# A message-passing layer: full tables carry their surplus rows into the next table, keys of pairs are computed earlier, and leftovers of pairs are ranked in front of the next group's second layer

## The chip, the cores and the metric

The kernel runs on one core of one Trainium2 chip. The metric is the device time in microseconds (us) of one execution. Besides the tensor engine (PE, whose loading of weights is listed as PEld), the core has the vector engine (DVE), the scalar engine (ACT), GpSimd (POOL) and the queue engine SP, which here only issues transfers. Every engine works through its own instructions strictly in order, and engines wait for each other on semaphores. Transfers are issued from SP, ACT and POOL.

## The reference, cut to what matters

```python
h = jnp.maximum(_layernorm(x, axis=-1), 0.0)              # x: 12500 x 128
# inside the layer; idx_i = src (unsorted), idx_j = dst (sorted), 400000 edges
h = h @ W_in2f.T
Wij = smu(f_ij @ W_f1.T + b_f1) @ W_f2.T + b_f2            # f_ij: 400000 x 20
Wij = Wij * rcut_ij[:, None]
x_ij = h[idx_j] * Wij                                      # one message of 128 numbers an edge
agg = jax.ops.segment_sum(x_ij, idx_i, num_segments=h.shape[0])
out = smu(agg @ W_o1.T + b_o1) @ W_o2.T + b_o2             # added to x
```

Each edge makes a message from the node row at its `dst` end and from a two-layer filter of its 20 attributes; messages are summed at the `src` end. Edges come sorted by `dst`, so the rows to gather lie close together, and the places to sum into are scattered.

## The kernel before, in words

Edges are cut into 3125 tiles of 128; four tiles are a **group** (782 groups), two groups a super-group. The main loop takes one step a group and is software-pipelined: step p does for group p+1 the second layer (`weigh`, on PE, tile `pw`) and the product with the gathered rows (`mix`, on DVE, tile `ms`), for p+2 the gather by one-hot product (`gather` on PE, `take` on ACT, tile `hg`), and for p+3 the first layer (`hide`, `bend`). The order on each engine is the order in which the code names the calls; nothing reorders it.

**Slots.** The messages are not summed at once. They are scattered into a table in device memory and read back. Nodes are cut into 98 bins of 128 nodes; a table has `CAP` rows for each bin, each of 129 floats: the message and the node's place in its bin. Row by row, the slot is the count of earlier rows of the same bin: `bins` marks and adds counts (DVE), `count` forms running counts by products with triangular matrices (PE, tile `pc`), `read` takes them out (DVE), `number` adds the bin's start to give the index `ix` (DVE). `places_in` (ACT, L1086) writes the places into the last column of `ms`. Then POOL issues one indirect transfer for each tile of 128 rows (`scatter_rows`, L1110). A message tile is reused once its transfers have landed; there are 9 of them.

**Pairs.** In about every 2.5th group the four tiles are taken as two against two. `number` makes `key` for them (L812), `spread_keys` turns two of its columns on PE (L830), `match` compares (DVE, L838), and rows of the same bin are put side by side by a product (`permute`, PE, L875), so that one descriptor writes two rows: 2 transfers instead of 4. What found no partner is ranked by `rank_left` (PE, L848 and L849) and `place_left` (DVE, L855 and L856), packed into one tile `lt`, and sent with a later **host** group as a fifth transfer, whose bins are counted there too (`bins`, L724 and L725).

**Epochs.** The groups are cut into ten epochs (`PARTS`, in super-groups), each with its own table. During an epoch, the table of the epoch before is fetched from SP (`fetch`, L1141, four chunks ahead), a one-hot is built of the place column (`choose`, DVE, L1155), and each 128 rows are multiplied by it (`add`, PE, L1168), a bin's products accumulating; `Q` = CAP/128 such slices a bin, summed into `agg`. Three stores in memory are used in turn. A store has to hold zeros, or rows that cannot be mistaken, where nothing was written: before their first use the parts of the bins that may stay empty are filled with zeros (`clear`, L226, from SP), and reuse is told apart by an offset added to the places (`mark_round`). The tables are sized so that each alone holds its fullest bin: CAP is 768, 768, 768, 768, 640, 512, 384, 384, 256, 128, thus Q is 6, 6, 6, 6, 5, 4, 3, 3, 2, 1, 42 in all.

The groups of the last two epochs are computed in between the others (every ninth super-group, from the second epoch on) and kept in memory; they are scattered at the very end from these rows (`kept_rows`). An alarm count (`bad`) sends the program into a slow general path if a table was too small.

## Time and profile before

| what | value |
|---|---|
| median of 3 runs | 3832.49 us (3823.35 to 3832.53) |
| the profiled execution, as a whole | 3826.85 us |
| its span, first to last instruction | 3825.1 us |
| mean granted clock of PE | 0.964 |
| PE, PEld, DVE, ACT, POOL busy | 3294.2, 2872.9, 3116.8, 2839.2, 2855.5 us |
| device memory read, written | 500.66 MB, 398.23 MB |
| scatters (indirect transfers from POOL) | 2902 |

Times in the trace are of the span. A busy share is an average over all stages; a wait is listed with what ended it last. In the groups of instructions the columns are busy time, mean ns of one, and the engine's idle time before them with what ended it. Matmuls overlap, so the mean of one is longer than what it adds to the engine's busy time. Scatters in order show where the epochs lie: the first scatter of the second epoch starts at 614 us, of the third at 1189, of the fourth at 1735 and of the fifth at 2282 us.

### The profile page before, as it was taken

What the parts mean: (1) busy time and instruction counts of PE and PEld (TensorE: products, weight loads), DVE (VectorE), ACT (ScalarE), POOL (GpSimd) and SP (SyncE); (2) the same over time, 40 slices, a digit from 0 to 9 for tenths busy, and PEclk for the clock granted to TensorE, in tenths of its full rate; (3) what the DMA queues carried; (4) which work ended last, traced back from release to release, by engine and by line L of the source; (5) the groups of instructions that cost most, each with busy time, mean ns of one, the idle gap of its engine ahead of it and who ended that gap; (6) DMA issues with size and microseconds to landing.
All of it is one profiled execution on the core that took longest, in us unless ns stands there. A gap on an engine that the chain in (4) does not pass through costs nothing.

```text
span 3825.1 us, 90354 instructions
## 1 busy us (share of the span) xinstructions
PE 3294.2 (86%) x28066; PEld 2872.9 (75%) x28066; DVE 3116.8 (81%) x8275; ACT 2839.2 (74%) x7986; POOL 2855.5 (75%) x2946
## 2 busy tenths in 40 slices
PE   8777776988888999999989889999999889997767
PEld 4346665877777888878878778888888888887657
DVE  7878976877777888888888888888898888886657
ACT  7767766878888888888888888888778777875102
POOL 6777777777767777777777777777777777777776
PEclk9989988999999999999999999999999999999889
DMA  5888888888888878888878878888888888886977
GB/s 156 231 236 239 236 230 233 248 251 246 263 253 232 238 227 231 244 239 235 229 222 232 235 214 242 253 239 247 232 244 249 233 235 246 241 236 177 312 247 228
DMA packets 663936, 905.06 MB, mean 237 GB/s; under 512 B 179875, under 2 KB 462631, under 8 KB 663321
## 3 DMA queue, kind: packets, MB, share of 16 engines
q1 hardware_dynamic: 556025, 666.99, 63.5%
q0 software_dynamic: 100112, 219.93, 17.8%
q10 hardware_dynamic: 7312, 12.29, 0.9%
q8 instruction: 228, 3.74, 0.4%
q14 instruction: 259, 2.12, 0.2%
HBM read 500.66 MB, written 398.23 MB: 235 GB/s over the span
## 4 chain that ended last, share of the span: by engine, by line
PE 33%; DMA 18%; DVE 16%; ACT 11%; issue 11%; POOL 9%; SPq 2%; ACTq 0%; DVEq 0%; POOLq 0%
DMA buf<-ms,ix 12%; PE pg L1168 10%; POOL buf L1110 9%; PE pw L998 6%; PE pt L875 5%; ACT hg L973 3%; PE pc L752 3%; DVE se L1155 3%; DVE mt L838 2%; DVE ms L1040 2%; ACT oh L634 2%; ACT ge L926 2%; PE ph L954 2%; PE pw L1000 1%; DVE pc L796 1%
## 5 line engine op out<-in xcount | busy, mean ns | idle before, releaser
L1110 POOL DMA_INDIRECT buf<-ms,ix x2516 | 2444.3, 971 | 813.6 <-issue 569.0
L1168 PE MATMUL pg<-se,rw 128*128 128x128 f32 x8036 | 1168.7, 284 | 107.8 <-DVE se L1155 61.2
L1168 PEld LDWEIGHTS pg<-se,rw 128*128 128x128 f32 x8036 | 1037.2, 194 | 166.4 <-issue 65.5
L973 ACT ACTIVATE hg<-ph,w_sb 128x128 f32<-128x128 f32 x2784 | 781.9, 361 | 94.5 <-PE ph L954 80.4
L998 PE MATMUL pw<-w_f,ge 128*128 128x128 f32 x5568 | 779.2, 284 | 30.5 <-DVE ms L1040 14.3
L998 PEld LDWEIGHTS pw<-w_f,ge 128*128 128x128 f32 x5568 | 697.5, 197 | 50.0 <-issue 23.7
L1155 DVE TENSOR_TENSOR se<-irow_ps,rw 128x1536 f32<-128x1536 f32 (+1 forms) x345 | 587.4, 1703 | 112.1 <-DMA rw<-buf 89.5
L634 ACT ACTIVATE oh<-rbc,nrow 128x512 bf16<-128x512 uint8 x725 | 538.6, 743 | 33.5 <-DMA rbc<-rel_dram 33.1
L635 ACT ACTIVATE oh<-oh,onesb 128x512 bf16<-128x512 bf16 x743 | 536.0, 721 | 24.2
L796 DVE TENSOR_REDUCE pc<-pc 128x4 f32<-128x392 f32 (+1 forms) x782 | 466.4, 596 | 81.0 <-PE pc L752 77.4
L1040 DVE TENSOR_TENSOR ms<-pw,hg 128x512 f32<-128x512 f32 x482 | 330.2, 685 | 137.8 <-DMA buf<-ms,ix 36.5
L875 PE MATMUL pt<-ms,mt 128*128 128x129 f32 x2676 | 345.0, 279 | 55.0 <-DVE at L855 48.2
L875 PEld LDWEIGHTS pt<-ms,mt 128*128 128x128 f32 x2676 | 319.1, 193 | 66.7 <-issue 23.3
L752 PE MATMUL pc<-eo,tri 128*128 128x392 f16 x782 | 261.5, 334 | 69.8 <-DVE ix L818 46.8
L954 PE MATMUL ph<-hw,oh 126*128 126x128 bf16 x2784 | 274.4, 221 | 39.0 <-ACT hg L973 36.0
L926 ACT ACTIVATE ge<-pu 128x512 f32<-128x512 f32 x451 | 272.9, 605 | 17.4 <-PE pu L918 15.5
L752 PE MATMUL pc<-so,ones_h 128*128 128x392 f16 (+1 forms) x996 | 279.4, 306 | 0.1
L1000 PE MATMUL pw<-wls,f 128*128 128x128 bf16 x2784 | 274.2, 222 | 0.0
L1088 ACT ACTIVATE ms<-lo_b,mark 128x4 f32<-128x4 uint8 x309 | 91.3, 295 | 231.9 <-DVE ms L1040 219.7
L1110 POOL DMA_INDIRECT buf<-lt,ix x214 | 203.3, 950 | 78.0 <-issue 27.7
L954 PEld LDWEIGHTS <-oh 126*128 126x128 bf16 x2784 | 217.0, 99 | 52.5 <-issue 44.3
L752 PEld LDWEIGHTS <-ones_h 128*128 128x128 f16 x1554 | 151.8, 98 | 139.2 <-issue 17.1
(344 smaller groups left out, 5313.0 us busy)
## 6 DMA issues: line engine op xcount, KB each, us to landing
rw<-buf SPq DMA_DIRECT2D x292, 774.0 KB
f<-f_parts SPq DMA_DIRECT2D x370, 240.0 KB
buf<-zero SPq DMA_DIRECT2D x146, 387.0 KB
rbc<-rel_dram SPq DMA_DIRECT2D x389, 128.0 KB
buf<-ms,ix POOLq DMA_INDIRECT x2516
f_parts<-hs SPq DMA_DIRECT2D x105, 360.0 KB
rw<-buf SPq DMA_DIRECT2D x49, 645.0 KB
f_parts<-hs SPq DMA_DIRECT2D x107, 240.0 KB
```

Source lines behind the costliest of these rows:

```text
L634: nc.scalar.activation(oh, loaded[s][1][:, o:o + n], AF.Abs, bias=pneg if s < FEW // SUP else nrow)
L635: nc.scalar.activation(oh, oh, AF.Relu, scale=-1.0, bias=onesb[:, 0:1])
L752: nc.tensor.matmul(to, by, of, start=start, stop=stop, skip_group_check=True)
L796: nc.vector.tensor_reduce(sl[:, :n], pc[:, :n], op=ALU.max, axis=AX.X)
L875: nc.tensor.matmul(po[:, j * (ROW + 1):j * (ROW + 1) + w], pp[:, o:o + P], ms[:, i, ROW:ROW + w], start=(i == 0), stop=(i == 1))
L954: nc.tensor.matmul(ph[:, j * P:(j + 1) * P], oh[:3 * WIN, a:a + P], hw[:3 * WIN, g % PER, :], start=True, stop=True)
L973: nc.scalar.activation(hg[:, j * P:(j + 1) * P], rows_of[g][:, j * P:(j + 1) * P], AF.Copy, scale=w_sb[:, t + j:t + j + 1])
L998: nc.tensor.matmul(pw[:, a:a + P], ge[:, a:a + P], w_f2, start=(a == 0), stop=False, skip_group_check=True)
L1040: nc.vector.tensor_tensor(ms[:, :n, 0:P], pw.rearrange("p (j f) -> p j f", f=P)[:, :n], hg.rearrange("p (j f) -> p j f", f=P)[:, :n], op=A ...
L1110: i = nc.gpsimd.indirect_dma_start(out=(wide if g in host or g in pair_no else bufs)[k][:, :], out_offset=bass.IndirectOffsetOnAxis(ap=ix, ...
L1155: nc.vector.tensor_tensor(se[:, a:a + n], own.unsqueeze(1).to_broadcast([P, n, P]), rows_in[c][:, a:a + n, P:P + 1].to_broadcast([P, n, P] ...
L1168: nc.tensor.matmul(pgs[0][:, g, :], rows_in[c][:, o, 0:P], sel[c][:, o, :], start=(q == 0), stop=(q == Q[k] - 1))
```

## The change

**Tables.** The ten tables are now chains (`CHAINS`, of 5, 3, 1 and 1). In a chain, a bin's part of table k+1 lies right behind its part of table k in one store (`store`, 98 bins of S = 3200 rows). A bin that is full in epoch k goes on in the rows of table k+1: the slot is limited by `LIM`, the room of both tables, and the counts of the next epoch begin with what went over (`carry`, from one more product in `limits_of`). So only the end of a chain has to hold the fullest bin. CAP becomes 640, 640, 640, 640, 640, 512, 384, 384, 256, 128 and Q 5, 5, 5, 5, 5, 4, 3, 3, 2, 1, 38 in all; `PARTS` is rebalanced. The first five tables have rows of their own and are all cleared before use, 192, 192, 192, 256 and 256 rows a bin (before: three tables, 384 rows a bin each), each within the first three quarters of the epoch before it. The second chain reuses the rows of the first three tables. Waits between scatters, clears and fetches are now given by hand (`apart`, `behind_all`).

**Pairs.** `number` of a pair runs right behind `read` in the step before. `rank_left` and `place_left` of a pair run in the following step, in front of `weigh` and behind it. `rank_left` has one more product, which adds the constant `spot`, so that the subtraction L855 is gone; the comparison now reads `falling` and the product's bank. In a host group, one scalar-tensor-tensor operation takes the place of L724 and L725. Pairs are 224 instead of 223, scatters 2901 instead of 2902.

**Message tiles.** A plain group's tile is now made as 128 x 4 x 129 (`message_tile`) and a pair's as 128 x 2 x 259 (`pair_tile`); before, one flat tile was viewed in both ways.

```diff
-PARTS = (59, 58, 58, 58, 47, 37, 27, 24, 16, 7)
+PARTS = (58, 55, 54, 53, 48, 42, 33, 25, 16, 7)
+CHAINS = (5, 3, 1, 1)
...
+    for i, n in enumerate(CHAINS):
+        a = len(CAP)
+        ends = [0]
+        for k in reversed(range(a, a + n)):
+            ends.insert(0, max(ends[0] + 1, math.ceil(sum(rows_for(k, a + n)) / P)))
+        caps = [(u - v) * P for u, v in zip(ends, ends[1:])]
+        at_ = 0 if i <= 1 else OFF[-1] + CAP[-1]
+        for j, c in enumerate(caps):
+            CAP.append(c)
+            OFF.append(at_ + sum(caps[:j]))
+            LIM.append(c + (caps[j + 1] if j + 1 < n else 0))
...
+    store = dram.tile([NB + SPARE, S, ROW], F32, name="buf")
+    rows_at = store.rearrange("b s r -> (b s) r")
...
             if g in first:
-                nc.vector.memset(before, 0.0)
+                if carried(first[g]):
+                    nc.vector.tensor_scalar(before, carry, BIG, None, op0=ALU.min)
+                else:
+                    nc.vector.memset(before, 0.0)
...
                 if g in host:
-                    lot = cnt.tile([P, NB], F16, name="el")
                     rows_of_bins(k)
-                    nc.vector.tensor_scalar(lot, bin_row, left_of[host[g]][1], None, op0=ALU.is_equal)
-                    nc.vector.tensor_add(then, whole, lot)
+                    lot = then
+                    nc.vector.scalar_tensor_tensor(then, bin_row, left_of[host[g]][1], whole, op0=ALU.is_equal, op1=ALU.add)
...
+                if carried(k + 1):
+                    on_one = bank_of[:, 1, :NB]
+                    nc.tensor.matmul(on_one, one_h, after, start=True, stop=True)
+                    nc.vector.tensor_scalar(carry, on_one, -float(CAP[k]), 0.0, op0=ALU.add, op1=ALU.max)
...
-            nc.tensor.matmul(at_, tri, met_of(g, 0, 2), start=True, stop=False, skip_group_check=True)
+            nc.tensor.matmul(at_, ident, spot, start=True, stop=False, skip_group_check=True)
+            nc.tensor.matmul(at_, tri, met_of(g, 0, 2), start=False, stop=False, skip_group_check=True)
             nc.tensor.matmul(at_[:, 1:2], ones_h, met_of(g, 0), start=False, stop=True, skip_group_check=True)
...
-            at_ = cnt.tile([P, 2], F32, name="at")
-            nc.vector.tensor_tensor(at_, spot, kt[:, 2 * P:2 * P + 2], op=ALU.subtract)
             nc.vector.tensor_tensor(pp[:, 4 * P:].rearrange("p (j e) -> p j e", j=2),
-                                    irow_ps.unsqueeze(1).to_broadcast([P, 2, P]),
-                                    at_.unsqueeze(2).to_broadcast([P, 2, P]), op=ALU.is_equal)
+                                    falling.unsqueeze(1).to_broadcast([P, 2, P]),
+                                    kt[:, 2 * P:2 * P + 2].unsqueeze(2).to_broadcast([P, 2, P]), op=ALU.is_equal)
...
         def message_tile():
-            return msg.tile([P, 2 * (2 * ROW + 1)], F32, name="ms")
+            return msg.tile([P, GRP, ROW], F32, name="ms")
...
+        def pair_tile():
+            return msg.tile([P, 2, 2 * ROW + 1], F32, name="ms")
...
+                for j in range(FIRST):
+                    if (j == 0 and g >= BY) or 0 < j <= k or (j == k + 1 and is_clean(g)):
+                        behind_all(i, after_clear[j])
+                    else:
+                        apart(i, f"cleared{j}")
...
-            elif k + 1 < BUFS:
+            elif k + 1 < FIRST and cleared < len(cleans):
                 past = BY if k == 0 else 0
-                upto = min(len(cleans), -(-(i + 1 - past) * len(cleans) // (ng - 4 - past)))
+                upto = min(len(cleans), -(-(i + 1 - past) * len(cleans) // (by_group[k] - g0 - 2 - past)))
...
             step()
-            number(at(p + 1))
+            if at(p + 1) not in paired:
+                number(at(p + 1))
+            if g in paired:
+                rank_left(g)
             weigh(at(p + 1))
+            if g in paired:
+                place_left(g)
...
             read(at(p + 2))
+            if at(p + 2) in paired:
+                number(at(p + 2))
             parts(hi)
-            if at(p + 1) in paired:
-                rank_left(at(p + 1))
-                place_left(at(p + 1))
```

How the rows of the program stand now, at three places. A row is line, operation, written tile and what it reads, and what it waits for; `DMASW` are landings of POOL's transfers, `DMAHW` of SP's and ACT's, the others are engines. First ACT, around two plain groups and a pair. Before:

```order
L1036 ACTIVATE ms<-lo_b 128x2x2 [waits DMASW6_49,DMASW5_49,DVE_49]
L1037 ACTIVATE ms<-hic,shift 128x2
L973 ACTIVATE hg<-ph,w_sb 128x128 [waits PE_49]
L973 ACTIVATE hg<-ph,w_sb 128x128 x3
L926 ACTIVATE ge<-pu 128x512 [waits PE_49]
L634 ACTIVATE oh<-rbc,nrow 128x512 [waits DMAHW4_49]
L635 ACTIVATE oh<-oh,onesb 128x512 [waits Activation_49]
L1180 ACTIVATE agg<-pg_15306 128x512 [waits PE_49]
L1090 ACTIVATE ms<-lo_b 128x4 [waits DMASW2_49,DMASW1_49,DMASW7_49,DMASW0_49,DVE_49]
L973 ACTIVATE hg<-ph,w_sb 128x128 [waits PE_49]
```

and now:

```order
L1059 ACTIVATE ms<-lo_b 128x2x2 [waits DMASW3_49,DMASW2_49,DVE_49]
L1060 ACTIVATE ms<-hic,shift 128x2
L1000 ACTIVATE hg<-ph,w_sb 128x128 [waits PE_49]
L1000 ACTIVATE hg<-ph,w_sb 128x128 x3
L953 ACTIVATE ge<-pu 128x512 [waits PE_49]
L644 ACTIVATE oh<-rbc,nrow 128x512 [waits DMAHW7_49]
L645 ACTIVATE oh<-oh,onesb 128x512 [waits Activation_49]
L1113 ACTIVATE ms<-lo_b 128x4 [waits DMASW6_49,DMASW7_49,DMASW5_49,DMASW4_49]
L1000 ACTIVATE hg<-ph,w_sb 128x128 [waits PE_49]
L1000 ACTIVATE hg<-ph,w_sb 128x128 x3
```

The places of a plain group (L1090 and L1088 before, L1113 and L1111 now) no longer wait for DVE, whose product fills the other columns of the same tile; those of a pair (L1036, now L1059) still do. Before, 474 of the 567 such instructions of plain groups wait for DVE; now none of 566.

Second, DVE around one pair: `key` is the pair's key, L1031 or L1053 its product, L838 or L866 the matching. Before:

```order
L796 TENSOR_REDUCE pc<-pc 128x4 [waits PE_49]
L1645 TENSOR_TENSOR hs<-sm,hs 120x512 [waits DMAHW6_49,DMAHW5_49,Activation_49]
L812 SCALAR_TENSOR_TENSOR key<-pc,hic 128x4 [waits DVE_49]
L1031 TENSOR_TENSOR ms<-pw,hg 128x2x2x128 [waits DMASW4_49,DMASW5_49,PE_49,Activation_49]
L838 SCALAR_TENSOR_TENSOR mt,met<-pt,key,onesb 128x256 [waits DVE_49,PE_49]
L838 SCALAR_TENSOR_TENSOR mt,met<-pt,key,onesb 128x256
...
L796 TENSOR_REDUCE pc<-pc 128x4 [waits PE_49]
L1155 TENSOR_TENSOR se<-irow_ps,rw 128x1536 [waits DMAHW2_49,PE_49]
L855 TENSOR_TENSOR at<-spot,pt 128x2 [waits PE_49]
L856 TENSOR_TENSOR mt<-irow_ps,at 128x256 [waits DVE_49]
L818 SCALAR_TENSOR_TENSOR ix<-pc,hic 128x4
```

and now:

```order
L824 TENSOR_REDUCE pc<-pc 128x4 [waits PE_49]
L840 SCALAR_TENSOR_TENSOR key<-pc,hic 128x4 [waits DVE_49]
L1053 TENSOR_TENSOR ms<-pw,hg 128x2x2x128 [waits DMASW1_49,DMASW2_49,PE_49,Activation_49]
L866 SCALAR_TENSOR_TENSOR mt,met<-pt,key,onesb 128x256 [waits DVE_49,PE_49]
L866 SCALAR_TENSOR_TENSOR mt,met<-pt,key,onesb 128x256
L730 SCALAR_TENSOR_TENSOR so_177<-es,so_177 128x98
L824 TENSOR_REDUCE pc<-pc 128x4 [waits PE_49]
L846 SCALAR_TENSOR_TENSOR ix<-pc,hic 128x4 [waits DMASW3_49,DVE_49]
L883 TENSOR_TENSOR mt<-falling,pt 128x256 [waits PE_49]
L1214 TENSOR_TENSOR se<-irow_ps,rw 128x1280 [waits DMAHW4_49,PE_49]
```

The key stands directly behind the reading of the counts, with no other work between; the ranks' comparison (L883) is one row, behind the next group's index, and the one-hot (L1214) has 1280 columns instead of 1536.

Third, SP in the third epoch, between two fetches of `rw`. Before:

```order
L1141 DMA rw<-buf_64 128x2x774 [waits DMAHW2_49,PE_49]
L588 DMA f_140<-f_parts 120x1024 [waits DMAHW3_49]
L604 DMA rbc<-rel_dram 128x1024 [waits DMAHW4_49,Activation_49]
...
L619 DMA hw<-h_dram 126x1x128 [waits DMAHW5_49]
...
L619 DMA hw<-h_dram 126x1x128 [waits DMAHW6_49]
L1633 DMA sm<-in_f_t 120x1x512 [waits DMAHW7_49]
L1141 DMA rw<-buf_64 128x2x774 [waits DMAHW0_49,DVE_49,PE_49]
```

and now:

```order
L1200 DMA rw<-buf 128x2x645 [waits DMAHW0_49,PE_49]
L598 DMA f_143<-f_parts 120x1024 [waits DMAHW1_49]
L614 DMA rbc<-rel_dram 128x1024 [waits DMAHW2_49,Activation_49]
...
L629 DMA hw<-h_dram 126x1x128 [waits DMAHW3_49]
...
L629 DMA hw<-h_dram 126x1x128 [waits DMAHW4_49]
L237 DMA buf<-zero 64x2x387 [waits DMAHW5_49]
L237 DMA buf<-zero 64x2x129 [waits DMAHW6_49]
L1200 DMA rw<-buf 128x2x645 [waits DMAHW7_49,PE_49]
```

The fetches are 645 instead of 774 floats a partition and bin, and clears, two transfers for two bins, now stand between them in epochs that had none.

196 lines of the change are left out of this document (113 added, 83 removed).

## The prediction

> **What bounds the kernel now.** I read the busy shares first; they name no winner.
>
> ```profile
> PE 3294.2 (86%) x28066; PEld 2872.9 (75%) x28066; DVE 3116.8 (81%) x8275; ACT 2839.2 (74%) x7986; POOL 2855.5 (75%) x2946
> ```
>
> POOL looks as idle as any. But what did it wait for? The answer on its scatters alone, with its idle time by cause, and then the same scatters by stretch (columns: length, POOL busy and count, granted clock of PE, share of the transfer engines, GB/s):
>
> ```profile
> L1110 POOL DMA_INDIRECT buf<-ms,ix x2516: 952/958/1520, 13.0 to 3544.0; - x194
>   issue: 644.3, 2111
> ...
> 13.00:200.00 187.00, 135.55 (x140) 0.95 0.72 198
> 200.00:600.00 400.00, 297.24 (x303) 0.90 0.82 234
> 600.00:1200.00 600.00, 432.56 (x447) 0.96 0.87 250
> 1200.00:3400.00 2200.00, 1672.11 (x1728) 0.99 0.83 236
> 3400.00:3765.00 365.00, 277.31 (x287) 0.90 0.80 245
> ```
>
> A scatter is busy 0.96 us, and before 2111 of them stands "issue", 0.305 us each (644.3/2111): POOL waits for nobody, it just cannot issue sooner. So a scatter costs 1.27 us whatever else happens: 2200/1728 = 1.273 from 1200 to 3400 us, 365/287 = 1.272 behind it. **From 1200 us to the last scatter POOL is full**, and nothing that makes PE, DVE or ACT lighter can shorten that stretch. By the same 1.273 us, 447 scatters need 569 us where 600 passed, 303 need 386 of 400, 140 need 178 of 187. The time that can be had is 31 us in 600:1200, 14 us in 200:600, and 9 us in the start, which this change does not touch.
>
> Why is POOL short of work in the second epoch (614 to 1189 us) and not in the third, which has the same arithmetic? All engines over the second, third and fourth epochs, and then waits and groups of the second against the third:
>
> ```profile
> 614.00:1189.00 575.00, 490.48 (x4281) 436.78 (x4281) 442.21 (x1195) 460.94 (x1315) 413.63 (x427) 0.96 0.87 252
> 1189.00:1735.00 546.00, 496.61 (x4450) 442.23 (x4449) 466.98 (x1240) 468.34 (x1340) 414.88 (x430) 1.00 0.83 233
> 1735.00:2282.00 547.00, 494.00 (x4380) 440.87 (x4379) 456.73 (x1225) 462.82 (x1296) 415.48 (x430) 0.98 0.81 228
> ```
>
> The second epoch's waits:
>
> ```profile
> ACT ms L1090 <- DVE ms L1040: 37.4, 31, 8.7
> POOL buf L1110 <- ACT ms L1090: 22.7, 14, 5.1
> PEld pg L1168 <- ACT agg L1180: 19.9, 12, 3.3
> POOL buf L1110 <- DVE ix L821: 14.5, 6, 4.7
> DVE se L1155 <- DMA rw<-buf: 13.2, 2, 8.6
> PE pt L830 <- DVE key L812: 12.4, 10, 6.3
> ACT oh L634 <- DMA rbc<-rel_dram: 11.1, 5, 7.0
> ```
>
> The third epoch's rows for the two that waited for transfers:
>
> ```profile
> L634 ACT ACTIVATE oh<-rbc,nrow 128x512 bf16<-128x512 uint8 x133 | 98.9, 744 | 0.2 <-DMA rbc<-rel_dram 0.2
> L1155 DVE TENSOR_TENSOR se<-irow_ps,rw 128x1536 f32<-128x1536 f32 x51 | 89.2, 1749 | 2.8 <-PE pg L1168 2.8
> ```
>
> 575 us against 546 for nearly as many scatters (427 and 430). Waits for transfers, 13.2 + 11.1 us, are 0.2 us in the third epoch. What differs is traffic:
>
> ```profile
> DMA packets 97033, 144.79 MB, mean 252 GB/s; under 512 B 28189, under 2 KB 64531, under 8 KB 96960
> rw<-buf SPq DMA_DIRECT2D x49, 774.0 KB
> buf<-zero SPq DMA_DIRECT2D x48, 387.0 KB
> ...
> DMA packets 85969, 127.45 MB, mean 233 GB/s; under 512 B 28423, under 2 KB 52895, under 8 KB 85893
> ```
>
> The first three rows are the second epoch's, the last the third's: 17.3 MB more, about the 48 clears of 387 KB (19 MB).
>
> **The change part by part.** The prices, from the groups by shape:
>
> ```profile
> L1168 PE MATMUL pg<-se,rw 128*128 128x128 f32 x8036 | 1168.7, 284 | 107.8 <-DVE se L1155 61.2 <-DVE agg L1182 26.0 <-ACT agg L1180 19.8
> L1155 DVE TENSOR_TENSOR se<-irow_ps,rw 128x1536 f32<-128x1536 f32 x292 | 511.0, 1750 | 107.3 <-DMA rw<-buf 87.7 <-PE pg L1168 18.9 <-DMA rbc<-rel_dram 0.3
> L1155 DVE TENSOR_TENSOR se<-irow_ps,rw 128x1280 f32<-128x1280 f32 x49 | 72.6, 1482 | 4.8 <-PE pg L1168 2.8 <-DMA rw<-buf 1.8
> L855 DVE TENSOR_TENSOR at<-spot,pt 128x2 f32<-128x2 f32 x214 | 32.0, 150 | 4.6 <-PE pt L849 4.0
> L724 DVE TENSOR_SCALAR el<-mv,lat 128x98 f16<-128x98 f32 x214 | 65.5, 306 | 0.3
> L725 DVE TENSOR_TENSOR so<-so,el 128x98 f16<-128x98 f16 x214 | 45.5, 213 | 7.3
> L714 DVE SCALAR_TENSOR_TENSOR so<-es,so 128x98 f16<-128x98 f16 x223 | 57.8, 259 | 3.7
> L848 PE MATMUL pt<-met,tri 128*128 128x2 f16 x192 | 32.1, 167 | 27.0 <-DVE mt L838 25.3
> L1088 ACT ACTIVATE ms<-lo_b,mark 128x4 f32<-128x4 uint8 x309 | 91.3, 295 | 231.9 <-DVE ms L1040 219.7 <-DMA buf<-ms,ix 8.6 <-issue 1.4
> ```
>
> *Fewer slices.* Four tables lose one slice a bin: 4 x 98 = 392 products at 0.145 us of PE (1168.7/8036; the mean of 284 ns overlaps its neighbours), 57 us in all, 14 us an epoch. The one-hots fall from 1.750 to 1.482 us, 49 an epoch: 13 us of DVE. Each fetched table is smaller by 129/774, or 6.5 MB.
>
> *Pairs and hosts.* DVE saves 0.150 (L855) and, in the host, 0.306 + 0.213 - 0.259 (the one operation priced as L714), 0.41 us for each of 35 pairs in the second epoch: 14 us. PE gains one product with two columns, for which no row exists; bounds 0.10 to 0.30 us, between a bare step of the array and a whole float product. I take L848's 0.167: 6 us an epoch. The early key removes most of the 12.4 us for which PE waited for L812. The ranks stand where they stood on PE, right in front of `weigh`; on DVE the comparison goes behind the next index, so up to 0.2 us later, ahead of a `permute` that has `weigh` and slices in front of it. I count it as nothing; without that cover it is 35 x 0.2 = 7 us an epoch.
>
> *Tiles of their own shape.* In the order of rows, ACT's places of a plain group no longer wait for DVE. ACT stood 37.4 us for this in the second epoch alone, 219.7 us at L1088. It stands in front of the gathered rows of the group after next, and POOL's 22.7 us of waiting ends on it. This is the part that I would have missed in the diff.
>
> *Clears.* 192 instead of 384 rows a bin: 9.5 MB less in the first and second epochs each. The second epoch falls to 144.8 - 9.5 - 6.5 = 129 MB, the amount of the third, which is full. But the third and fourth get clears that they never had, 256 rows a bin or 13 MB: 127.5 + 13 - 6.5 = 134 MB. SP gets 98 transfers more in each, at this row's median of 0.447 us some 44 us:
>
> ```profile
> L226 SPq DMA_DIRECT2D buf<-zero x147: 377/447/3212, 47.4 to 1139.6; - x147
> ```
>
> By the second epoch's price (29 us for 17.3 MB, 1.7 us a MB), 6.5 MB would cost the third and fourth 11 us each. Against that stand 27 us less DVE and 8 us less PE an epoch, ACT's freedom, and nine message tiles, some 40 us of scatters, in hand. I take zero, bounds 0 and 11 each. In the first epoch the clears of the next table are squeezed into 35 groups instead of 62, about 21 more there on SP: up to 9 us against the 14 us to be had; I take a gain of 4. The alarm products and carries are a few instructions an epoch, under 1 us each. Scatters of plain groups now wait for DVE beside ACT and a landing; how many waits stand before a scatter does not matter from 1200 to 3400 us, where those that end on a landing stand as long as the others:
>
> ```profile
> POOL buf L1110 <- issue: 389.7, 1276, 0.8
> POOL buf L1110 <- DMA buf<-ms,ix: 36.0, 118, 0.3
> ```
>
> *The sum,* against the profiled execution of 3826.85 us (its span of 3825.1 and 1.75 around it, which stay): second epoch, DVE 27, PE 8 and about 24 of waits for transfers are more than the 31 us that POOL can give, but the waits of PE for L1180 (19.9 us, sums of the first table copied by ACT) partly stay: -25. First epoch -4. One scatter fewer -1.3. From 1200 us on: 0. That is 3796.5. The profiled execution lies 5.6 us under the median of 3832.49 and inside its runs' 3823.35 to 3832.53, so I add half of that: **3799 us**, by itself 3788 to 3814.
>
> **The rivals.**
>
> *All gaps close.* The first epoch fills too: 45 + 1.3 off 3826.85, **3781 us**. For it: its POOL waits also end on ACT. Against: SP's squeeze there.
>
> *Given back.* The third and fourth epochs pay 11 us each by the MB and the first gains nothing: 3826.85 - 25 + 22 - 1 = **3823 us**, no change that shows.
>
> *The second epoch's shortfall was something else* (the ACT copies, the clock) and stays: **3826 us**.
>
> *The queue decides, slower.* If the second epoch starves not by MB but by the number of clears queued on SP ahead of loads, halving their size gains nothing there (still 49), and the third and fourth, with 98, lose at least its 31 us each: 3826.85 + 62 = **3889 us**. It decides once SP issues later than the three super-groups by which loads run ahead. Against: in the first epoch SP sends a clear in four of five groups, and POOL loses only 14 us of 400.
>
> *The clock.* The granted clock is 0.90 in the stretch where PE has least to do and 0.99 where POOL is full; here with PE's busy time first:
>
> ```profile
> 200.00:600.00 400.00, 292.39 (x2253) 234.03 (x2252) 324.96 (x993) 278.04 (x813) 297.24 (x303) 0.90 0.82 234
> 1200.00:3400.00 2200.00, 2020.29 (x18213) 1822.78 (x18211) 1890.53 (x4970) 1814.09 (x5120) 1672.11 (x1728) 0.99 0.83 236
> ```
>
> If less work drew the clock to 0.90 throughout, PE would need 2020.3 x 0.99/0.90 = 2222 us of a stretch of 2200, become the bound there and eat the gain elsewhere: 3826.85 + 22 = **3849 us**. Against: PE loses 1 or 2%, and 73% and 92% busy lie 9 points of clock apart, so under one point is to be expected. The Trainium skill ("TensorE: Matmul & The Clock Gate", Part 1: The HAM clock gate) says that the array's clock is throttled by default, and that recent activity releases it; by that rule taking products away speaks against the change. The trace agrees in direction, and no run here shows the size.
>
> *That it doesn't do what it says* would need a full pair of tables and the slow path; the rows of the program show Q of 5, and a chain's end has the old margin.
>
> **How the numbers follow.** Forecast 0.60, all gaps 0.12, given back 0.13, something else 0.05, the queue 0.07, the clock 0.03. About 0.3%, 11.5 us, is what a measurement of this kernel tells from no change: faster means under 3821, slower over 3844. Faster 0.72, the same 0.18, slower 0.10. The range reaches from all gaps closed to no gain, 3780 to 3827; above it lie the two slow rivals.
>
> **What would show it.** Between 600 and 1200 us the scatters should come to about 468 (600/1.273 is 471); from 1200 on still 1.27 us apart, with no POOL wait over 1 us in the third and fourth epochs. L1168's products should be 392 fewer, DVE some 140 us lighter, ACT's wait for DVE in front of the places nearly gone, while the span falls by less than a quarter of DVE's saving. Transfers of 0.87 and more in the third and fourth epochs with gaps at POOL would speak for the give-back, an SP that is never idle there for the queue. It is wrong outright if POOL leaves its 1.27 us anywhere behind 1200 us, or if a scatter itself becomes cheaper or dearer.

## The result: slower, 3862 us where 3799 were forecast

The changed kernel takes 3861.75 us (median of 4 runs, 3856.38 to 3869.99). The kernel before, on the same chip, takes 3831.08 us (4 runs, 3823.35 to 3832.53). The ratio is 1.0088, with a 95% interval of 1.0074 to 1.0103: 31 us slower. The forecast was 25 to 30 us faster, its range ended at 3827, and slower had a chance of 0.10.

The same view as in the prediction shows where the time went: the scatters by stretch, with POOL's busy time and their number. First before, with the stretch behind 1200 us cut at 2100 us, where the epochs of the surplus chain end.

```profile
1200.00:2100.00 900.00, 683.94 (x707) 0.99 0.82 232
2100.00:3400.00 1300.00, 988.17 (x1021) 0.99 0.84 239
```

And now:

```profile
200.00:600.00 400.00, 286.86 (x291) 0.88 0.75 203
600.00:1200.00 600.00, 456.42 (x470) 0.97 0.85 236
1200.00:2100.00 900.00, 650.30 (x670) 0.96 0.86 237
2100.00:3400.00 1300.00, 989.18 (x1021) 0.99 0.81 230
```

At 1.273 us a scatter, as before, these counts tell nearly all of it. Between 600 and 1200 us 470 scatters went out instead of 447: 29 us won, and the stretch is full (600/1.273 is 471). Between 2100 and 3400 us there are 1021, as before. But between 1200 and 2100 us, where POOL had been full with 707, there are 670: 47 us lost. Between 200 and 600 us it is 291 instead of 303: 15 us lost. The start won 2 scatters. The balance, 47 + 15 - 29 - 3 = 30 us, comes close to the 32 us by which the profiled spans differ (3857.0 and 3825.1 us).

Work that the change should remove, it removed. The 392 products of the sums that the code leaves out are 784 rows fewer in the trace, which has two for each product (8036 before, 7252 now), and the busy time of this line fell from 1168.7 to 1083.2 us. DVE's busy time went from 3116.8 to 3021.4 us:

```profile
PE 3265.7 (85%) x27445; PEld 2857.4 (74%) x27758; DVE 3021.4 (78%) x7859; ACT 2810.9 (73%) x7992; POOL 2864.1 (74%) x2946
...
L1227 PE MATMUL pg<-se,rw 128*128 128x128 f32 x7252 | 1083.2, 285 | 104.0 <-DVE se L1214 61.2 <-DVE agg L1241 23.4 <-ACT agg L1239 15.6
```

This profile lacks some products on PE: 27445 stand beside 27758 weight loads, so PE's 3265.7 us are too low. The profile of e1 below, with the same products, has all 27758 and 3284.0 us, 10 us less than before. So DVE, ACT and PE do less, POOL sends one scatter fewer, and the kernel takes longer. What it waits for in the bad stretch stands in the view of waits between 1300 and 2100 us (us in total, times, longest):

```profile
ACT hg L1000 <- PE ph L981: 81.9, 45, 15.3
...
ACT oh L644 <- DMA rbc<-rel_dram: 36.0, 14, 7.9
...
POOL buf L1133 <- ACT ms L1113: 32.9, 24, 4.8
...
PE pt L902 <- DVE mt L883: 25.0, 17, 13.6
...
DVE se L1214 <- DMA rw<-buf: 10.6, 1, 10.6
...
PE pt L858 <- DVE key L840: 2.7, 6, 0.9
```

The same waits of the kernel before, between 1300 and 2100 us:

```profile
PE pt L830 <- DVE key L812: 15.1, 15, 2.2
ACT hg L973 <- PE ph L954: 14.5, 22, 1.2
...
PE pt L875 <- DVE at L855: 9.1, 11, 1.9
...
ACT oh L634 <- DMA rbc<-rel_dram: 0.2, 1, 0.2
```

ACT builds the one-hots (L644) from the index rows `rbc`, which SP loads, and these rows now come late: 36.0 us instead of 0.2. And PE stands in front of the permuting products (L902) until DVE has compared the ranks of what is left (L883): 25.0 us, where before it waited 9.1 us for L855. But 13.6 of the 25.0 us are one wait, and it too goes back to a late load: the 10.6 us for which DVE waits for `rw`, the first rows of the next table, end at 1700.7 us, L883 comes behind them on DVE, and PE's wait ends at 1703.4 us. SP had sent this load at 1692.4 us, behind four clears. The other 16 waits are 11.4 us, hardly more than before. The early key did what it was made for: PE's wait for it fell from 15.1 to 2.7 us.

What else SP does there is in the views of its clears: number, shortest, median and longest ns on SP. Before, none were sent in these epochs. Now, from 1140 to 2060 us:

```profile
L237 SPq DMA_DIRECT2D buf<-zero x192: 495/642/1656, 1142.8 to 2041.5; - x192
```

By the median this is 192 x 0.642 = 123 us of SP's time in 920. The prediction had priced 98 an epoch at 0.447 us, 44 us; two epochs of it would be 88. Added up in the trace from 1200 to 1500 us, all of SP's instructions take 263 of the 300 us now (272 transfers among them) and took 203 before (214 transfers).

### The profile page after: what moved, and what is told of

Same layout as the page of the kernel before. It is cut to its first block, busy times and chain, and to the rows that moved or that the text cites. A ratio compares the mean times of both kernels' runs of the same rounds, so it can differ in the third digit from the quotient of the medians.

```text
span 3857.0 us, 89326 instructions
## 1 busy us (share of the span) xinstructions
PE 3265.7 (85%) x27445; PEld 2857.4 (74%) x27758; DVE 3021.4 (78%) x7859; ACT 2810.9 (73%) x7992; POOL 2864.1 (74%) x2946
## 4 chain that ended last, share of the span: by engine, by line
PE 30%; DMA 16%; DVE 13%; ACT 8%; issue 8%; POOL 7%; SPq 2%; DVEq 0%; ACTq 0%; POOLq 0%; another core or an unknown queue 0%
DMA buf<-ms,ix 9%; PE pg L1227 8%; POOL buf L1133 7%; PE pw L1025 7%; PE pt L902 6%; ACT hg L1000 3%; PE pc L767 3%; DMA rbc<-rel_dram 2%; DVE mt L866 2%; PE ph L981 2%; PE pw L1027 2%; ACT oh L644 1%; DVE se L1214 1%; DVE pc L824 1%; DMA f<-f_parts 1%
## 5 line engine op out<-in xcount | busy, mean ns | idle before, releaser
L1227 PE MATMUL pg<-se,rw 128*128 128x128 f32 x7252 | 1083.2, 285 | 104.0 <-DVE se L1214 61.2
L1000 ACT ACTIVATE hg<-ph,w_sb 128x128 f32<-128x128 f32 x2784 | 786.9, 363 | 409.9 <-PE ph L981 384.6
L1227 PEld LDWEIGHTS pg<-se,rw 128*128 128x128 f32 x7252 | 950.6, 194 | 154.8 <-issue 54.6
L1214 DVE TENSOR_TENSOR se<-irow_ps,rw 128x1280 f32<-128x1280 f32 (+1 forms) x345 | 535.4, 1552 | 126.8 <-DMA rw<-buf 100.5
L644 ACT ACTIVATE oh<-rbc,nrow 128x512 bf16<-128x512 uint8 x726 | 540.6, 745 | 51.7 <-DMA rbc<-rel_dram 51.7
L902 PE MATMUL pt<-ms,mt 128*128 128x129 f32 (+1 forms) x2688 | 364.5, 288 | 108.5 <-DVE mt L883 91.4
L902 PEld LDWEIGHTS pt<-ms,mt 128*128 128x128 f32 x2688 | 333.3, 199 | 128.6 <-issue 63.5
L981 PE MATMUL ph<-hw,oh 126*128 126x128 bf16 x2784 | 277.4, 223 | 61.0 <-ACT hg L1000 56.6
L981 PEld LDWEIGHTS <-oh 126*128 126x128 bf16 x2784 | 219.1, 99 | 75.0 <-issue 66.3
L767 PE MATMUL pc<-so,ones_h 128*128 128x392 f16 x782 | 261.6, 335 | 0.0
L681 DVE TENSOR_TENSOR eo<-irow_ps,ed 128x784 f16<-128x784 f16 (+1 forms) x391 | 217.0, 555 | 24.3 <-ACT ed L671 24.3
L1027 PEld LDWEIGHTS <-f 128*128 128x128 bf16 x2784 | 220.8, 100 | 9.4
```

The costliest lines, as they stand in the source:

```text
L644: nc.scalar.activation(oh, loaded[s][1][:, o:o + n], AF.Abs, bias=pneg if s < FEW // SUP else nrow)
L767: nc.tensor.matmul(to, by, of, start=start, stop=stop, skip_group_check=True)
L902: nc.tensor.matmul(po[:, j * (ROW + 1):j * (ROW + 1) + w], pp[:, o:o + P], ms[:, i, ROW:ROW + w], start=(i == 0), stop=(i == 1))
L981: nc.tensor.matmul(ph[:, j * P:(j + 1) * P], oh[:3 * WIN, a:a + P], hw[:3 * WIN, g % PER, :], start=True, stop=True)
L1000: nc.scalar.activation(hg[:, j * P:(j + 1) * P], rows_of[g][:, j * P:(j + 1) * P], AF.Copy, scale=w_sb[:, t + j:t + j + 1])
L1027: nc.tensor.matmul(pw[:, a:a + P], fb[:, o + a:o + a + P], wls, start=False, stop=(a + P == n), skip_group_check=True)
```

## The experiments

Three theories stood at the start. *Queue:* SP has no time left to issue, and the number of clears decides. *Traffic:* the bytes of the clears decide. *Order:* the new place of the pairs' keys and ranks (and the tiles) delays the messages. Runs of the kernel before beside them had medians of 3831.0 to 3832.5 us. The last three columns are numbers of scatters, from the view shown above. A profile is of one execution, and not always of a typical one: those of e1 (3837.95 us) and e11 (3818.30 us) are the longest of their runs, those of e2, e3, e5, e9 and e12 the shortest. So the times are the firmer evidence, and a difference of a few scatters says little.

| run | us | ratio to before, interval | 200:600 | 600:1200 | 1200:2100 |
|---|---|---|---|---|---|
| before | 3831.08 | | 303 | 447 | 707 |
| the change | 3861.75 | 1.0088 (1.0074 to 1.0103) | 291 | 470 | 670 |
| e1_one_transfer | 3830.42 | 0.9995 (0.9985 to 1.0005) | 288 | 469 | 690 |
| e2_double_bytes | 3861.86 | 1.0088 (1.0067 to 1.0109) | 292 | 469 | 671 |
| e3_split_table_2 | 3877.27 | 1.0128 (1.0108 to 1.0149) | 290 | 461 | 671 |
| e4_spread_first | 3862.86 | 1.0085 (1.0059 to 1.0111) | 294 | 464 | 670 |
| e5_order_back | 3855.11 | 1.0059 (1.0040 to 1.0079) | 292 | 472 | 679 |
| e6_order_back_one_transfer | 3820.80 | 0.9970 (0.9958 to 0.9982) | 288 | 471 | 698 |
| e7_flat_tiles | 3875.28 | 1.0111 (1.0083 to 1.0139) | 288 | 465 | 669 |
| e8_fewer_transfers | 3820.97 | 0.9970 (0.9954 to 0.9986) | 295 | 471 | 695 |
| e9_double_table_2 | 3895.02 | 1.0175 (1.0148 to 1.0203) | 292 | 449 | 666 |
| e10_tiles_alone | 3821.16 | 0.9979 (0.9967 to 0.9992) | 303 | 455 | 706 |
| e11_order_back_fewer | 3809.41 | 0.9946 (0.9925 to 0.9967) | 296 | 470 | 699 |
| e12_order_fewer_spread | 3805.02 | 0.9941 (0.9920 to 0.9962) | 306 | 471 | 699 |

### The number of transfers

Tables 3 and 4 get 256 rows a bin, 4 rows a partition on 64 partitions, and the tile of zeros holds 3: hence two transfers for two bins. On 128 partitions it is 2 rows and one transfer.

```
-        m = (CAP[k] - z) * ROW // ZP
+        zp = P if k >= 3 else ZP
+        m = (CAP[k] - z) * ROW // zp
```

> The clears of tables 3 and 4 go out as one transfer for two bins (128 partitions of 258 floats a bin) instead of two (64 partitions of 387 and of 129): the same bytes, 49 transfers a table instead of 98. Queue theory (SP has no time left to issue: it is 87 to 90% busy where POOL stands, 84% or less where it doesn't): SP loses some 12 issues of 0.65 us per 100 us, POOL's waits of 46 us between 1300 and 2100 us shrink to under 10, about 3822 us (3810 to 3835). Traffic theory (the 13 MB an epoch are what costs): unchanged, 3862 us within 8. Order theory (the ranks, keys and tiles of pairs make the scatters late): unchanged, 3862 us.

Measured: 3830.42 us, 31 us less, as long as the kernel before. From 1140 to 2060 us SP now spends 98 x 0.450 = 44 us on clears instead of 123, because the number is halved and because a transfer on 128 partitions takes SP less time than one on 64:

```profile
L238 SPq DMA_DIRECT2D buf<-zero x98: 409/450/3361, 1146.7 to 2017.9; - x98
```

From 1200 to 1500 us its instructions add up to 243 us. In the waits between 1300 and 2100 us the late index rows fell from 36.0 to 9.4 us, and the wait for the ranks stayed:

```profile
PE pt L903 <- DVE mt L884: 22.0, 18, 9.8
...
ACT oh L645 <- DMA rbc<-rel_dram: 9.4, 8, 3.6
```

That speaks for the queue, by the same bytes, and also by the same number of pieces: two bins are 256 contiguous runs of memory either way. Number and shape changed together here. In the profiled execution, the longest of ten, 17 of the 37 lost scatters stay lost (690, not 707).

The counterpart doubles the number where nothing was lost, on the same 64 partitions. The same bytes now lie in twice as many pieces, too.

```
-        for o, w in chunks(m, zero.shape[1] // n):
+        for o, w in chunks(m, 2 * ROW if k == 2 else zero.shape[1] // n):
```

> The clears of table 2 alone (sent in the second epoch, where the change loses nothing) go out as two transfers for two bins, the same bytes. Queue theory: the second epoch gets 49 more issues and loses what the third and fourth lose, 15 to 25 us: 3877 to 3887 us, gaps at POOL between 600 and 1100 us. Traffic theory and order theory: unchanged, 3862 us within 8.

Measured: 3877.27 us, 15.5 us more, with 461 scatters between 600 and 1200 us instead of 470. The number of transfers costs, shown from both sides; that it is the number of pieces is spoken against by e1, and by e8 below, which sends more pieces in fewer transfers and gains. Traffic and order predicted no change here and fall as sole causes.

### The bytes

e2 keeps e1's 98 transfers and covers 512 rows of a bin instead of 256, from the same zeros read once for each bin.

```
-        z = 0 if b == NB - 1 else ZMIN[k]
+        z = 0 if b == NB - 1 else ZMIN[k] - 256 * (k >= 3)
```

> As e1_one_transfer, but each of its clears of tables 3 and 4 covers 512 rows of a bin instead of 256 (the rows below are overwritten by messages anyway): twice the bytes, 49 transfers a table. Queue theory: the same time as e1_one_transfer within 10 us, some 3822. Traffic theory: 13 MB more in each of two epochs at 1.7 us a MB, 44 us above e1_one_transfer, some 3906 us. Order theory: as e1_one_transfer.

Measured: 3861.86 us, 31 us above e1 for 26 MB, 1.2 us a MB. SP's time hardly moves (98 transfers at a median of 452 ns), but the index rows are late again:

```profile
ACT oh L649 <- DMA rbc<-rel_dram: 34.2, 12, 7.6
```

So the queue theory as the only one falls too. Number and bytes both cost, and the symptom is the same: rows that SP loads come late. That in e1 and e3 they are issued late, and in e2 wait behind transfers that are still moving bytes, is the likely reading; no run here shows the way of a single load.

e9 does the same in the second epoch, where the change had halved the clears: 384 rows a bin for table 2, as before the change.

```
-        z = 0 if b == NB - 1 else ZMIN[k]
+        z = 0 if b == NB - 1 else ZMIN[k] - 192 * (k == 2)
```

> The changed kernel with table 2's clears (second epoch) covering 384 rows of a bin instead of 192, as many as before: 9.5 MB more, the same 50 transfers. The bytes' reading: e2_double_bytes lies 31 us above e1_one_transfer for 26 MB, 1.2 us a MB, so 11 us more, 3873 us, with gaps at POOL in 600 to 1200 us (by the forecast's 1.7 us a MB 16 us, 3878). If only the number of transfers costs: 3862 us within 6.

Measured: 3895.02 us, 33 us more, and 449 scatters between 600 and 1200 us, which is the 447 of before. Its waits from 620 to 1140 us show the late rows:

```profile
ACT hg L1004 <- PE ph L985: 49.0, 33, 4.2
...
ACT oh L648 <- DMA rbc<-rel_dram: 30.6, 13, 9.3
POOL buf L1137 <- ACT ms L1117: 24.6, 20, 6.1
```

Of ACT's 30.6 us for `rbc` the changed kernel, in the same view, has 0.2:

```profile
ACT oh L644 <- DMA rbc<-rel_dram: 0.2, 1, 0.2
```

The 9.5 MB cost 3.5 us each here, three times what a MB cost in e2 and twice the forecast's 1.7. The 11 to 16 us that were expected are half of that or less: the price of a byte isn't the same in the two places. What sets them apart wasn't tried.

### The order of pairs, and the tiles

e5 puts the keys and ranks of pairs back to their old places.

```
-            if at(p + 1) not in paired:
-                number(at(p + 1))
-            if g in paired:
-                rank_left(g)
+            number(at(p + 1))
             weigh(at(p + 1))
-            if g in paired:
-                place_left(g)
...
-            if at(p + 2) in paired:
-                number(at(p + 2))
             parts(hi)
+            if at(p + 1) in paired:
+                rank_left(at(p + 1))
+                place_left(at(p + 1))
```

> The changed kernel with the keys and ranks of pairs at the places they had before (key behind the next group's transfers, ranks and their comparison at the end of a group's turn); all else stays. The first epoch's gaps at POOL stand one at each pair (every 16 us from 414 to 499 us) and the product behind the comparison of the ranks ends them. Order theory: these 18 to 25 us between 300 and 500 us go, and a part of the 46 us between 1300 and 2100 us: 3830 to 3842 us. Queue theory: the gaps stay, 3862 us within 8. A third reading, that the order is what filled the second epoch: 10 to 30 us come back between 600 and 1200 us, 3872 to 3892 us.

Measured: 3855.11 us, 6.6 us less, short of the order theory's 20 to 30 and inside the queue theory's 3862 within 8. Beside the kernel before, its interval overlaps that of the change, so this run alone hardly shows a gain. The second epoch stays full (472), so the third reading falls. The first epoch doesn't move (292). In the waits between 1300 and 2100 us, that of L902 for L883 has fallen to 0.4 us, while others grew:

```profile
ACT hg L1000 <- PE ph L981: 56.6, 46, 3.4
ACT oh L644 <- DMA rbc<-rel_dram: 55.7, 22, 7.4
...
PE pt L858 <- DVE key L840: 19.5, 18, 4.4
```

PE now waits 19.5 us for the key instead of 2.7, and ACT 55.7 us for the index rows instead of 36.0. That ACT comes to these rows earlier because PE is free of L883, so that one stall stood in the shadow of the other, is a reading and not shown. It led to the next run, where the order should be worth more with e1's transfers under it.

> The edits of e1_one_transfer and e5_order_back together. If the clears' transfers and the order each cost their own part: 3830 less what e5_order_back gains, 3800 to 3810 us. If the order was a gain: over 3840 us. If both only fight for the same waits: 3825 to 3832 us.

Measured: 3820.80 us, 9.6 us below e1; 698 scatters between 1200 and 2100 us, and the late index rows at 18.6 us. It lies in none of the three ranges, between the first and the third. Its interval is clear of e1's, so the old order is worth some 10 us here. Whether it is worth more than beside the change isn't shown: 6.6 and 9.6 us don't differ clear of the noise.

e7 puts one flat tile under both shapes of messages.

```
         def message_tile():
-            return msg.tile([P, GRP, ROW], F32, name="ms")
+            return msg.tile([P, 2 * (2 * ROW + 1)], F32, name="ms")[:, :GRP * ROW].rearrange("p (j r) -> p j r", r=ROW)
```

> The changed kernel with one flat message tile under both shapes, as before, so that ACT's places of plain groups wait for DVE's product again. Forecast's reading (ACT's freedom is a gain): ACT stands 200 us at the places again, POOL's gaps grow, 3870 to 3885 us. Rival (ACT only moves its wait from the places to PE's gathered rows, 94 us of waiting there before and 410 after): 3862 us within 8.

Measured: 3875.28 us, 13.5 us more, in the range of the forecast's reading and outside the rival's, that ACT only moves its wait. The rival is right in part: ACT's waits for DVE in front of the places come back with 302 us over the whole run, and its waits for the gathered rows fall from 385 to 184 us. But POOL's waits that end on L1113 grow from 46 to 97 us. The intervals of e7 and of the change overlap, so the gain of the tiles rests on the next run as well. The other way round, the kernel before with this one edit:

> The kernel before with one edit: message tiles of their own shape for plain groups and for pairs, so that ACT's places of plain groups don't wait for DVE. If the tiles gain by themselves what e7_flat_tiles lost (13.5 us): 3814 to 3821 us, and the gaps at POOL in 600 to 1200 us, 31 us before, shrink by as much. If they help only where clears crowd the other epochs: 3831 us within 6.

Measured: 3821.16 us, where the kernel before beside it took 3832.45: 11 us less by the medians, 3 to 13 by the interval of the ratio. Between 600 and 1200 us there are 455 scatters instead of 447. So the tiles are a gain, and some 8 of the 23 scatters that the second epoch won can be had by them alone.

### The first epoch, and a version faster than both

e4 spreads the clears of table 1 over 49 groups instead of 37.

```
         by_group = {k: eps_of[k][0] * PER + eps_of[k][1] * PER * 3 // 4 for k in range(FIRST - 1)}
+        by_group[0] = 99
```

> The clears of table 1 are spread over the groups 50 to 99 of the first epoch instead of 50 to 87. Queue theory: SP gets a clear in each group instead of four in three groups, the 25 us of gaps at POOL between 300 and 500 us fall to about 12: some 3849 us. Traffic theory: the same bytes over a longer stretch, also less loss, so this run doesn't tell the two apart. Order theory: unchanged, 3862 us within 8.

Measured: 3862.86 us, no change; 294 scatters instead of 291 in the first epoch, and 464 instead of 470 in the second. A miss for the queue theory as stated. e8 takes transfers away everywhere: three bins at a time, two rows a partition.

```
-    CB = 2
-    zero = const.tile([P, CB * 3 * ROW], F32, name="zero")
+    CB = 3
+    zero = const.tile([P, CB * 2 * ROW], F32, name="zero")
...
-        m = (CAP[k] - z) * ROW // ZP
+        zp = (CAP[k] - z) // 2 if z else P
+        m = (CAP[k] - z) * ROW // zp
```

> All clears go out as one transfer for three bins, two rows a partition (96 or 128 partitions): 34 a table instead of 50 or 99, the same bytes. Queue theory: e1_one_transfer took away 98 issues for 31 us; this takes away 75 more, most of them where POOL is full already, and a third of those at 300 to 500 us: 3815 to 3825 us. Traffic theory for what is left (the bytes cost 31 us for 26 MB in e2_double_bytes against e1_one_transfer): as e1_one_transfer, 3830 us within 6.

Measured: 3820.97 us, 9.5 us below e1, as the queue theory had it; but in the first epoch only 295. None of the three (order in e5, spread in e4, number here) moves the first epoch much by itself. Together with the order:

> The edits of e5_order_back and e8_fewer_transfers together. If each gains its own part as order did beside e1_one_transfer (9.6 us): 3809 to 3813 us. If what is left is the first epoch alone (18 us of gaps in e8_fewer_transfers) and neither edit reaches it: 3818 to 3822 us.

Measured: 3809.41 us, 11.6 us below e8, at the lower end of the first reading. With the spread as well:

> As e11_order_back_fewer, with table 1's clears spread over the groups 50 to 99 instead of 50 to 87. If in the first epoch the order and the loads behind the clears on SP hide one another (with the order back, ACT waits 16 to 26 us there for the rows that SP loads, which before that edit was 1 us), taking both away closes it: 3795 to 3803 us. If its gaps come from something else: as e11_order_back_fewer within 5 us.

Measured: 3805.02 us, faster than both kernels: 0.9941 of before (0.9920 to 0.9962), 57 us under the change. Its scatters, by stretch:

```profile
200.00:600.00 400.00, 301.81 (x306) 0.92 0.76 211
600.00:1200.00 600.00, 456.57 (x471) 0.97 0.86 242
1200.00:2100.00 900.00, 679.73 (x699) 0.98 0.89 246
```

That is 4.4 us below e11, outside the 3795 to 3803 us of the first reading and within the 5 us of the second, and the intervals of the two overlap. In its profile the first epoch is closed, 306 scatters against 296 in e11's; but e12's profile is of the shortest of six executions and e11's of the longest of five, 14.6 us apart. So that all three edits together close the first epoch is suggested and not shown.

### Key or ranks: left open

Which half of the new order costs these 10 us or so? Three kernels with e12's clears, for the early key alone, the early ranks alone, and both:

> As e12_order_fewer_spread (clears in 34 transfers a table, table 1's spread), with the early key of the change, but the ranks at their old place. If the key is the gain that the forecast took it for: 3797 to 3803 us against e12's 3805. If it does nothing where POOL is full: 3805 us within 4. If it is the key that delays the messages: 3810 to 3816 us.

> As e12_order_fewer_spread, with the ranks and their comparison in front of the next group's second layer as in the change, but the key at its old place. The permuting products wait for that comparison (25 us at their weights and products between 1300 and 2100 us in the changed kernel, none with the order back): 3811 to 3817 us. If the key and not the ranks costs: 3805 us within 4.

> As e12_order_fewer_spread with the order of the change. As much above e12 as e6 lay below e1 and e11 below e8, some 10 us: 3813 to 3818 us. If that came from the crowded loads alone and not from the order: 3805 us within 4.

These three ran where the kernel before itself took 5653.46 us (5615.91 to 5678.78, 27 runs), and so did a second set (before 5654.38 us):

> The kernel of e13_key_early again, for a chip on which the kernel before takes some 3831 us; what it tells is its ratio to the kernel before beside e12's 0.994 (3805 us). If the key is a gain: 3797 to 3803 us. If it does nothing where POOL is full: 3805 us within 4. If the key delays the messages: 3810 to 3816 us.

> The kernel of e14_ranks_early again, under the same condition. If the ranks' place costs: 3811 to 3817 us and waits of the permuting products for the comparison between 1300 and 2100 us; if the key costs: 3805 us within 4.

> The kernel of e15_both_early again, under the same condition: 3813 to 3818 us if the order costs some 10 us as it did beside e1 and e8, 3805 us within 4 if it does so only where loads are crowded.

Ratios to the kernel before there, first and second set: early key 0.9971 (0.9951 to 0.9991) and 0.9939 (0.9915 to 0.9963); early ranks 0.9966 (0.9943 to 0.9989) and 0.9931 (0.9906 to 0.9956); both 0.9934 (0.9912 to 0.9956) and 0.9903 (0.9875 to 0.9931). In both sets the change's order of both has the lowest ratio, against what e5, e6 and e11 say, but the intervals overlap, and e12 itself wasn't run there. And POOL isn't the bound there: between 600 and 1200 us e18 sends 310 scatters, and e12 471.

```profile
600.00:1200.00 600.00, 299.34 (x310) 0.80 0.52 147
```

So the six runs don't answer the question for the 3831 us in which it was asked, and it stays open whether the key or the ranks cost.

## Why the prediction was wrong, point by point

**What bounds the kernel: right.** The differences between the profiled spans follow from the numbers of scatters in each stretch at 1.273 us, to a few us. Where POOL stayed full, between 2100 and 3400 us, lighter sums and pairs won nothing: 1021 scatters before and now. Wrong was that POOL would stay full behind 1200 us whatever stood in front of the loads.

**The second epoch, -25 us: right, 29 us measured, and for the cause that was named.** e9 gives the bytes back and the scatters fall to 449. The prediction counted DVE's 27 us, PE's 8 and the waits for transfers together. With all the savings on DVE and PE in place, the bytes alone undo the gain, so those savings don't suffice. Whether they are needed wasn't tried. The tiles have a part (e10), which the sum didn't name; that 25 us came out so near is partly luck.

**Clears in the third and fourth epochs, "I take zero, bounds 0 and 11 each": the step that failed.** Measured are 47 us between 1200 and 2100 us, about 23 an epoch, twice the upper bound. Not all of it is the clears': by the profiles, e1 gives back 20 of the 37 scatters (25 us), the old order beside it 8 more (e6, 10 us), and 9 (11 us) stay lost. For these no run parts the cause; e2 shows that bytes cost in this stretch. Three errors lie in the step. First, the bound came from MB alone, while e1 shows 31 us for the number and the shape of the transfers at the same bytes, and e3 15.5 us for splitting them on the same partitions. Second, SP's price for a clear was taken from the row of before, 0.447 us on 128 partitions; on the change's 64 partitions it is 0.64. The row was of another shape: the lists of the order ahead of the prediction show the new clears on 64 partitions. Third, and worst, the zero was reached by setting DVE's 27 us, PE's 8 and ACT's freedom against it. Slack on those engines didn't pay for rows that arrive late: with DVE 95 us and ACT 28 us less busy than before, ACT still stood 36.0 us at L644 for `rbc`. The same lists showed the two clears standing in front of the next loads on SP.

**The ranks, "I count it as nothing; without that cover it is 35 x 0.2 = 7 us an epoch", and the early key as a gain: the order as a whole costs some 10 us, and its cause is open.** Taken back it is 6.6 us less beside the change, 9.6 beside e1 and 11.6 beside e8; of these, only that beside e1 is clear of the noise. The waits don't say why. Of PE's 25.0 us for L883 between 1300 and 2100 us, 13.6 end a stall that a late `rw` began (DVE's wait for it is 10.6 us here, 9.3 with the order back in e5, 6.7 in e1 and 2.7 in e8), and the other 16 waits have a mean of 0.7 us, against 0.8 for the 11 waits for L855 before. The key's wait fell by 12.4 us in the same stretch. The runs don't part key and ranks.

**ACT's freedom: right as a gain** (13.5 us in e7, 11 in e10, by the medians), though the wait `ACT hg L1000 <- PE ph L981` took over two thirds of it (201 of 302 us, e7 against the change).

**The prices on PE and DVE: off, without effect on the sum.** The 392 products were priced at 0.145 us, which is one row of the trace; a product has two rows, so that this price gives 114 us and not 57, and 85.5 us were measured. The product that adds `spot` takes 74.6 us for 215 pairs (L876), 0.35 us each, above its upper bound of 0.30. DVE became 95 us lighter, not some 140.

**The first epoch, -4 us: wrong by sign.** 12 scatters fewer, 15 us. "up to 9 us against the 14" saw SP's squeeze, but neither spreading the clears (e4) nor fewer of them (e8) nor the order (e5) cures it alone. The cause stays open; e12's profile suggests that it takes all three.

**The rivals.** "The queue decides" was nearest in mechanism, and its 0.07 was too low. Its half about the second epoch is refuted: halving the bytes did gain there at an unchanged number. Its half about the third and fourth is confirmed in direction, 23 us an epoch instead of 31. "Given back", by the MB, had the place right and the price too low. The clock fell from 0.99 to 0.96 in 1200:2100, but stayed at 0.99 in 2100:3400, where POOL is full with fewer products too, and e1 regains the time at 0.97: the rival of 0.90 throughout falls. Whether the lower clock only follows the stalls or adds to them wasn't parted. The prediction's own test, "wrong outright if POOL leaves its 1.27 us anywhere behind 1200 us", is what happened.

The Trainium skill ("DMA: Bandwidth & Descriptors", Issuing engines are not separate DMA queues) says that the time a sequencer takes to start a transfer is usually small beside the transfer. Taken alone, that would leave e1 and e3 without effect. They show 31 and 15.5 us, so here the sum isn't small: a queue that is given 272 transfers in 300 us and spends 263 us on its instructions has little left. For many small transfers the Trainium skill (the same page, Rules for kernel authors) advises one large one; that is what e1 and e8 do, and the times agree, 31 and 41 us below the change.

## What to carry to other kernels

When work is added to a queue that also loads what the critical engines need, price it by that queue's own time (number times the duration for the shape it will have) and by bytes, and don't set slack on other engines against it. A stretch that is full says nothing about how close its loads are to being late; ask which loads stand behind each added transfer. Before a long wait is put down to the instruction that ended it, follow that instruction's own wait back: more than half of the 25.0 us for the ranks began with one late load. And look where the profiled execution lies among its runs before counts from two profiles are compared.

## What the runs showed of the hardware

SP's time for a clear of two bins went by its shape and hardly by its bytes: medians of 0.66 us on 64 partitions for 387 floats a partition and bin, 0.61 for 129 and 0.66 for 774, and 0.45 us on 128 partitions for 258, for 387 (before) and for 516. The rows for e2 (1140 to 2060 us), and for table 2 in e9 with twice the bytes of the change (600 to 1140 us):

```profile
L242 SPq DMA_DIRECT2D buf<-zero x98: 332/452/2187, 1140.8 to 2039.1; - x98
```

```profile
L241 SPq DMA_DIRECT2D buf<-zero x51: 527/661/1740, 600.6 to 1008.3; - x51
```

And the same kernel can run in a wholly different condition. Beside e13 to e18 the kernel before took some 5654 us instead of 3831. In e18 ACT's, DVE's and POOL's own durations are as in e12, PE's granted clock is 0.82, and long idle times appear in front of instructions, for many of which the profile names no releaser on the core. The gathered rows on ACT, first in e12 and then in e18, the latter with the change's order and the same clears:

```profile
L1001 ACT ACTIVATE hg<-ph,w_sb 128x128 f32<-128x128 f32 x2784 | 784.7, 363 | 357.6 <-PE ph L982 334.8 <-DMA f<-f_parts 9.9 <-issue 7.3
```

```profile
L1001 ACT ACTIVATE hg<-ph,w_sb 128x128 f32<-128x128 f32 x2784 | 790.2, 366 | 1566.6 <-remote 656.0 <-PE ph L982 469.0 <-issue 215.3
...
L1134 POOL DMA_INDIRECT buf<-ms,ix x2514 | 2435.1, 969 | 1841.6 <-issue 1333.5 <-ACT hg L1001 161.1 <-ACT ge L954 100.0
```

One instruction takes 366 ns instead of 363, a scatter still 0.97 us, and yet ACT stands 1567 us in front of this line instead of 358. What holds the engines there wasn't found, so a ratio from this condition isn't carried over to the other.
